# Layer 0's self-attention in steps of two head pairs: a decoder kernel on Trainium2

## The chip, the cores and the metric

The kernel runs on one core of a Trainium2 chip, in one launch. The metric is the device time in microseconds. A core has five engines, each with its own queue of instructions that it works off in order: TensorE (PE, matrix products and transposes, which write into the PSUM banks), VectorE (DVE), ScalarE (ACT), GpSimd (POOL) and SyncE (SP, which issues DMAs). Engines wait for each other through semaphores.

## The reference, cut to what matters

Two decoder layers work on x of 16 x 256 x 128 (batch, tokens, width), each with a self-attention, a cross-attention to a context of 64 tokens and a mixture-of-experts block. All is float32. The change is in layer 0's self-attention, of 16 heads of 64:

```python
x = x + attn(layernorm(x))          # layer 0, self-attention
q, k, v = (x @ W).reshape(b, n, 16, 64)     # for Wq, Wk, Wv
bias = slope[h] * (pos[:, None] - pos[None, :])
scores = einsum('bihd,bjhd->bhij', q, k) * 64**-0.5 + bias
scores = where(pos[:, None] >= pos[None, :], scores, -1e30)
out = einsum('bhij,bjhd->bihd', softmax(scores), v)
attn = out.reshape(b, n, 1024) @ Wo + bo
...
x = x + xattn(layernorm(x), ctx)    # layer 0, leaky ReLU, norm, softmax, gate
x = x + moe(layernorm(x))           # layer 0, 8 experts, 2 per token
...                                 # layer 1, the same three kinds
```

## The kernel before

The tokens stand in eight chunks of 512, which is two batches each. Layer 0's self-attention is one loop over *head pairs*: 16 batches of 8 pairs are 128 units, and the loop has 134 steps. For PE, DVE and ACT the order of the instructions is the order of the code; POOL and SP follow by the same order where nothing else is said.

The stages of a unit and their lines (of the kernel before):

- `qk_mm` (L395) projects q or k for two pairs, one of the two in each step, four steps ahead of the scores. The product lies in a bank of the pool `ps_m` (tag "m", three banks); `qk_out` (L406, ACT) copies it out.
- `scores` (L450, PE): two heads side by side, each on 64 of the array's 128 rows. A head has a bank of `ps_s` (four banks). Only the causal three 128 x 128 blocks are made: one of 128 columns, one of 256.
- `greatest` (L463, DVE): adds the bias strip, writes the sum to SBUF and finds the extreme of each row. One step behind the scores.
- `exponentials` (L475, ACT) with the row sums. In the same step as greatest.
- `scaled`: reciprocal (L484, DVE), then two multiplications per head (L486, POOL). Two steps behind the scores.
- `flip` (L497, PE): three transposes per head, into an "m" bank; `flipped` (L502, DVE) copies them to SBUF. Four steps behind.
- `values` (L512, PE): the two heads on 64 of the array's columns each, into the one bank of `ps_o`; `values_out` (L524, ACT) copies the pair's 256 columns. Five steps behind.

Between them stand, in an order by hand, other pieces: `v_mm` and `v_out` (L412 PE, L421 DVE; v for eight heads and half the tokens), `y_mm` and `y_out` (L427, L435; the output projection of the batch before), `turn` and `turned` (L131, L385; the transposed layernorm of the next chunk), `stats` (L340, L341), `normed` (L346, L348, L354 on POOL) and `biased` (L376, POOL). q, k, v, y, turned layernorms, flips and the front pieces all draw on the three "m" banks in turn.

The *front pieces* of a chunk are the cross-attention, the router and the shared expert of layer 0 (`front_pieces`, L620 to L835). Each is a pair of a function for PE (or none) and one for the other engines (`mm`, `post`). They are planned one to a step from step 16 c + 22 for chunk c, so that the 28 pieces of a chunk overlap with those of the next; the first centring is L365 on ACT, the scatter of rows for the experts is L790 on POOL. The last pieces (chunk 7, part of chunk 6) run in the experts' loop that follows. The core of a step before, by engine:

```python
scores(at(0)); values(at(5)); flip(at(4), 0); flip(at(4), 1)    # PE, behind the pieces
greatest(at(1), 0); scaled(at(2), 0)                            # DVE, POOL
scaled(at(2), 1); greatest(at(1), 1)
flipped(at(4), 0); flipped(at(4), 1)
exponentials(at(1), 0); exponentials(at(1), 1); values_out(at(5))   # ACT
```

Of the kernel before, what the change touches and what calls it, by code (L numbers as in the profile page):

```python
# [15 lines left out]
F32 = mybir.dt.float32  # L16
# [6 lines left out]
P = 128  # L23
# [39 lines left out]
def kernel(ctx: ExitStack, tc: tile.TileContext, a: dict, out: bass.AP):  # L63
# [174 lines left out]
    with ExitStack() as ph:  # L238
# [162 lines left out]
        def qk_out(g, which):  # L401
            dst = qk[g, which] = qkvp.tile(
                [P, 2, N], F32, tag="qk"[which], name=f"{'qk'[which]}0_{g}", bufs=3
            )
            scale = (-(DH**-0.5), 1.0)[which]
            nc.scalar.activation(dst, m_of.pop(("qk", g, which)), AF.Copy, scale=scale)  # L406
# [83 lines left out]
        def flip(u, i):  # L490
            b, h = u[0], 2 * u[1] + i
            pr = pr_of.pop((b, h))
            ps = tp_of[b, h] = ps_m.tile([P, 3 * P], F32, tag="m", name=f"t0_{b}_{h}")
            for blk in range(3):

                cols = slice(blk * P, (blk + 1) * P)
                nc.tensor.transpose(ps[:, cols], pr[:, cols], ident)  # L497

        def flipped(u, i):
            b, h = u[0], 2 * u[1] + i  # L500
            pT_of[b, h] = pp.tile([P, 3 * P], F32, tag="pT", name=f"pT0_{b}_{h}", bufs=5)
            nc.vector.tensor_copy(pT_of[b, h], tp_of.pop((b, h)))  # L502

        def values(u):
            b, pair = u
            po = o_of[u] = ps_o.tile([P, N], F32, tag="o", name=f"o0_{b}_{pair}")
            v = vals[b, pair // 4]
            for jt, c0 in ((0, 0), (1, P)):
                for h in (2 * pair, 2 * pair + 1):
                    rows = slice((h % 2) * DH, (h % 2 + 1) * DH)  # L510
                    pT = pT_of[b, h]
                    nc.tensor.matmul(  # L512
                        po[rows, c0:N], v[:, jt, h % 8 * DH : (h % 8 + 1) * DH],
                        pT[:, 0:N] if jt == 0 else pT[:, N:],
                        start=(jt == 0), stop=(jt == 1),
                    )
            for h in (2 * pair, 2 * pair + 1):
                del pT_of[b, h]

        def values_out(u):  # L520
            b, pair = u
            if pair == 0:
                oT[b] = qkvp.tile([P, NPAIR, N], F32, tag="oT", name=f"oT0_{b}", bufs=1)
            nc.scalar.copy(oT[b][:, pair, :], o_of.pop(u))  # L524

# [68 lines left out]
        def front_pieces(c):  # L594
# [239 lines left out]
            def p_sdown():  # L834
                nc.vector.tensor_tensor(x[c], x[c], g.pop("sy"), ALU.add)  # L835

            first_part = [
                (None, lambda: stats(c, 0, "x0")),
                (None, lambda: stats(c, 2, "x0")),
                (None, lambda: root(c, "x0")),  # L840
                (None, p_centred),
                (mm_turn, p_turned),
                (mm_scores, p_leaky),
# [9 lines left out]
                (None, lambda: stats(c, 0, "f0")),  # L853
                (None, lambda: stats(c, 2, "f0")),
                (None, p_root2),
                (None, p_centred2),
                (mm_turn2, p_turned2),
                (mm_logits, p_logits),
# [84 lines left out]
        def early_pieces():  # L943
            def table():
                tiles_of("num_a", P - 1)
                starts_of("start_a", tabled["num_a"])

            def table2():
                start = tabled["start_a"]
                row = list(entries(tab_a, EARLY, start, None))[-1]  # L950
                nc.vector.tensor_copy(tab_a[:, 1, :], row)

                done = tabled["done"] = new("done", (P, E))
                nc.vector.tensor_scalar(done, start, -1.0, float(EARLY), ALU.mult, ALU.add)
# [36 lines left out]
        with tc.manual_schedule(engines=ordered):  # L991
            for t0 in (0, 2):
                stats(0, t0)
            normed(0, nc.vector)
            bias_strips()
            biased(0)
            turn(0)
            turned(0)
            for g in range(2):
                for which in range(2):  # L1000
                    qk_mm(g, which)
                    qk_out(g, which)
            front_constants()

            units = [(b, p) for b in range(B) for p in range(NPAIR)]
            n = len(units)
            side = {}  # L1010

            def plan(first, pieces):
                for k, piece in enumerate(pieces):
                    side.setdefault(first + k, []).append(piece)

            plan(17, [(lambda h=h: ctx_turn(h), lambda h=h: ctx_turned(h)) for h in range(2)])
            for c in range(NCHUNK):
                first_step = 16 * c + 22
                plan(first_step, front_pieces(c))
                if c == EARLY_C - 1:  # L1020
                    plan(first_step + 24, early_pieces())
                if c == NCHUNK - 1:
                    plan(first_step + 25, late_pieces())
            steps = 8 * (B - 1) + 14
            for i in range(steps):
                b, p = divmod(i, NPAIR)

                def at(lag):
                    return units[i - lag] if 0 <= i - lag < n else None

                pieces = []
                if i + 4 < n:
                    key = ((i + 4) // 2, i % 2)
                    pieces.append((lambda: qk_mm(*key), None, lambda: qk_out(*key)))
                if b < B and p in (2, 3, 6, 7):
                    vkey = (b, p // 4, p % 2)
                    pieces.append((lambda: v_mm(*vkey), lambda: v_out(*vkey), None))
                if p == 5 and 1 <= b <= B:
                    pieces.append((lambda: y_mm(b - 1), lambda: y_out(b - 1), None))
                if p == 7 and b % 2 == 0 and b // 2 + 1 < NCHUNK:  # L1040
                    c = b // 2 + 1
                    pieces.append((lambda: turn(c), None, lambda: turned(c)))
                more = side.get(i, [])

                for mm, _, _ in pieces:
                    mm()
                if at(0):
                    scores(at(0))
                if at(5):
                    values(at(5))  # L1050
                if at(4):
                    flip(at(4), 0)
                    flip(at(4), 1)
                for mm, _ in more:
                    if mm:
                        mm()

                if at(1):
                    greatest(at(1), 0)
                if at(2):  # L1060
                    scaled(at(2), 0)
                for _, out_v, _ in pieces:
                    if out_v:
                        out_v()
                if at(2):
                    scaled(at(2), 1)
                if at(1):
                    greatest(at(1), 1)
                if at(4):
                    flipped(at(4), 0)  # L1070
                    flipped(at(4), 1)
                if b % 2 == 0 and b // 2 + 1 < NCHUNK:
                    if p in (1, 3):
                        stats(b // 2 + 1, p - 1)
                    elif p == 4:
                        normed(b // 2 + 1)
                    elif p == 6:
                        biased(b // 2 + 1)

                if at(1):  # L1080
                    exponentials(at(1), 0)
                for _, _, out_a in pieces:
                    if out_a:
                        out_a()
                if at(1):
                    exponentials(at(1), 1)
                if at(5):
                    values_out(at(5))
                for _, post in more:
                    post()  # L1090


    pending = []
# [1073 lines left out]
```

## Time and profile before

| what | value |
|---|---|
| median of 3 runs | 1544.63 us (1543.79 to 1545.28) |
| the profiled execution | 1540.27 us |
| its span, first to last instruction | 1538.6 us |
| PE busy | 1461.4 us, 95% |
| DVE, ACT, POOL busy | 1175.6, 971.1, 667.9 us |
| mean granted PE clock | 0.982 |
| first and last scores of the attention (L450) | 18.0 us, 625.7 us |

The profile is of one execution. A row of the timeline gives the start, the time until the end of the last instruction merged in it, the engine, the line, the operation with its tiles (output <- inputs), the shape and the count; in brackets stands how long the engine was idle before it and what ended that. Matmuls are pipelined, so the distance of two starts tells what one costs, and the duration does not. PEld is PE's loading of weights.

A row of the view by stretches gives the stretch, its length, then the busy time and the number of instructions of PE, PEld, DVE, ACT and POOL, the granted clock, the share of the DMA engines and their GB/s.

### The profile page before, as it was taken

The page shows a single profiled execution, that of the slowest core. Times are in us where ns is not written, and L with a number is a line of the kernel's source. Part 1 is how long each engine was busy: PE and PEld are TensorE (multiplying, and loading weights), DVE is VectorE, ACT ScalarE, POOL GpSimd, SP SyncE. Part 2 cuts the span into 40 slices and gives each one's busy share as a digit, 9 for nine tenths or more (in the row PEclk, how much of TensorE's full clock was granted, in tenths as well). Part 3 has the DMA queues.
Part 4 walks back from the last instruction along what each step waited for, and adds up shares of the span by engine and source line. Part 5 has one row for each costly group of instructions (what it writes and reads, how often), then busy time and mean ns, then how long its engine had stood idle before and what let it go on. Part 6 is the DMA issues. An engine that isn't in the chain of part 4 may idle for free.

```text
span 1538.6 us, 34876 instructions
## 1 busy us (share of the span) xinstructions
PE 1461.4 (95%) x11569; PEld 1069.0 (69%) x11569; DVE 1175.6 (76%) x4620; ACT 971.1 (63%) x2619; POOL 667.9 (43%) x1102
## 2 busy tenths in 40 slices
PE   7999999999999999899999899999999996899897
PEld 4666666666666666689999777777777764565564
DVE  6666666667676767677878779999999978888863
ACT  5666565656565656354333368888888884767752
POOL 7354646464747464555533311101101015657643
PEclk9999999999999999999999989999999997999999
DMA  7760000000000000457777300000000000122122
GB/s 220 249 202 1 1 14 3 9 8 5 12 1 15 1 15 1 133 172 235 224 237 236 100 22 9 15 15 9 15 1 2 2 1 1 29 53 53 36 62 49
DMA packets 76321, 95.01 MB, mean 62 GB/s; under 512 B 15936, under 2 KB 59200, under 8 KB 76144
## 3 DMA queue, kind: packets, MB, share of 16 engines
q1 hardware_dynamic: 61312, 45.59, 10.9%
q10 hardware_dynamic: 10512, 38.28, 7.7%
q0 software_dynamic: 4320, 8.92, 1.7%
q8 instruction: 94, 1.54, 0.4%
q14 instruction: 83, 0.68, 0.1%
HBM read 64.11 MB, written 28.65 MB: 60 GB/s over the span
## 4 chain that ended last, share of the span: by engine, by line
PE 81%; DVE 12%; ACT 3%; issue 2%; DMA 1%; POOL 0%; POOLq 0%; ACTq 0%; SPq 0%; DVEq 0%
PE t L1659 7%; PE pqk L395 7%; PE s L450 6%; PE o L512 6%; PE t L497 5%; PE s L1627 5%; PE g L1298 4%; PE o L1674 4%; PE y L427 4%; PE y L1316 4%; PE u L1298 4%; PE pv L412 3%; PE pqk L1540 3%; PE yf L2035 2%; PE tx L1889 2%
## 5 line engine op out<-in xcount | busy, mean ns | idle before, releaser
L475 ACT ACTIVATE p<-p,nm 128x128 f32<-128x128 f32 (+1 forms) x512 | 227.5, 446 | 183.9 <-DVE nm L463 174.9
L486 POOL TENSOR_SCALAR p<-p,rs 128x128 f32<-128x128 f32 (+1 forms) x512 | 213.7, 434 | 187.3 <-DVE rs L484 159.4
L1649 ACT ACTIVATE p<-p,nm 128x256 f32<-128x256 f32 x512 | 225.7, 508 | 37.5 <-DVE nm L1638 35.2
L502 DVE COPY pT<-t 128x384 f32<-128x384 f32 x256 | 131.0, 553 | 102.4 <-PE t L497 102.3
L1638 DVE CUSTOM_DVE_ANT_0 p<-s,strip 128x256 f32<-128x256 f32 x512 | 188.1, 419 | 18.3 <-PE s L1627 17.8
L463 DVE CUSTOM_DVE_ANT_0 p<-s,strip 128x128 f32<-128x128 f32 (+1 forms) x512 | 158.1, 346 | 1.3 <-PE s L450 1.3
L1659 PEld LDWEIGHTS t<-ident,p 128*128 128x128 f32 x1024 | 111.2, 142 | 47.4 <-issue 12.6
L1659 PE MATMUL t<-ident,p 128*128 128x128 f32 x1024 | 141.5, 282 | 0.0
L1326 POOL DMA_INDIRECT rows_out<-yr,to x71 | 68.7, 967 | 117.3 <-DVE yr L1325 109.2
L1505 POOL TENSOR_SCALAR ve_a<-mv_a 128x2 f32<-128x2 f32 x16 | 3.7, 231 | 265.0 <-DVE mv_a L1500 264.9
L450 PE MATMUL s<-k,q 64*128 64x128 f32 (+1 forms) x1024 | 118.5, 350 | 0.0
L512 PE MATMUL o<-pT,v 128*64 128x256 f32 (+1 forms) x1024 | 112.8, 340 | 0.8 <-DVE pT L502 0.8
L497 PE MATMUL t<-ident,p 128*128 128x128 f32 x768 | 113.3, 283 | 0.2 <-ACT k L406 0.2
L450 PEld LDWEIGHTS s<-k,q 64*128 64x128 f32 x1024 | 67.0, 186 | 62.5 <-issue 56.3
L512 PEld LDWEIGHTS o<-pT,v 128*64 128x64 f32 x1024 | 62.9, 136 | 61.6 <-issue 25.9
L497 PEld LDWEIGHTS t<-ident,p 128*128 128x128 f32 x768 | 82.1, 141 | 23.2 <-issue 15.4
L475 ACT ACTIVATION_READ_ACCUMULATOR p<-p,nm 128x1 f32 x512 | 96.5, 188 | 0.0
L1306 ACT ACTIVATE gs<-gs 128x512 f32<-128x512 f32 x71 | 44.7, 630 | 77.0 <-DVE gs L1305 64.9
L1667 DVE COPY pT<-t 128x512 f32<-128x512 f32 x128 | 88.1, 688 | 6.2 <-PE t L1659 3.2
L1627 PE MATMUL s<-k,q 32*128 32x256 f32 x1024 | 85.3, 408 | 0.6 <-DVE nm L1638 0.5
L421 DVE COPY v<-pv 128x512 f32<-128x512 f32 x64 | 44.0, 687 | 50.8 <-PE pv L412 50.8
L790 POOL DMA_INDIRECT rows_in<-xn,slot_in x64 | 64.2, 1004 | 33.8 <-DVE nm L463 20.5
(338 smaller groups left out, 3487.8 us busy)
## 6 DMA issues: line engine op xcount, KB each, us to landing
gu<-in_L_ffn_gate_up_w ACTq DMA_DIRECT2D x71, 512.0 KB
rows_in<-zero SPq DMA_DIRECT2D x131, 130.0 KB
spread<-wrows SPq DMA_DIRECT2D x16, 512.0 KB
xr<-rows_in SPq DMA_DIRECT2D x71, 65.0 KB
y<-rows_out SPq DMA_DIRECT2D x16, 256.0 KB
x<-in_x SPq DMA_DIRECT2D x8, 256.0 KB
out_x<-yo SPq DMA_DIRECT2D x16, 128.0 KB
rows_out<-yr,to POOLq DMA_INDIRECT x71, 3.7
```

The source lines that it names most:

```text
L450: nc.tensor.matmul(ps_of[b, h][:, cols], q[rows, u2, iq], k[rows, u2, 0:nk], start=True, stop=True,)
L463: nc.vector.tensor_tensor_reduce(out=pr[:, cols], in0=ps[:, cols], in1=strip[:, h, P : 2 * P] if it == 0 else strip[:, h, :], scale=1.0, s ...
L475: nc.scalar.activation(pr[:, cols], pr[:, cols], AF.Exp, bias=nm[:, it : it + 1], scale=-1.0, accum_out=sm[:, it : it + 1],)
L486: nc.gpsimd.tensor_scalar(pr[:, cols], pr[:, cols], rs[:, it : it + 1], 1.0, ALU.mult, ALU.mult)
L497: nc.tensor.transpose(ps[:, cols], pr[:, cols], ident)
L502: nc.vector.tensor_copy(pT_of[b, h], tp_of.pop((b, h)))
L512: nc.tensor.matmul(po[rows, c0:N], v[:, jt, h % 8 * DH : (h % 8 + 1) * DH], pT[:, 0:N] if jt == 0 else pT[:, N:], start=(jt == 0), stop=(j ...
L1298: nc.tensor.matmul(ps[:, f, :], gu[:, lo + f * P : lo + (f + 1) * P], xT, start=True, stop=True,)
L1627: nc.tensor.matmul(ps_of[b, h][:, it, :], q[rows, g, it * P : (it + 1) * P], k[rows, g, :], start=True, stop=True,)
L1638: nc.vector.tensor_tensor_reduce(out=pr[:, it, :], in0=ps[:, it, :], in1=strip1[:, h, (1 - it) * P : (1 - it) * P + N], scale=1.0, scalar= ...
L1649: nc.scalar.activation(pr[:, it, :], pr[:, it, :], AF.Exp, bias=nm[:, it : it + 1], scale=-1.0)
L1659: nc.tensor.transpose(ps[:, jt, it * P : (it + 1) * P], pr[:, it, jt * P : (jt + 1) * P], ident,)
```

## The change

A step now takes two head pairs, that is four heads, and the loop has 67 steps. Both projections of q and k of the next but one step come first; then the scores of both pairs; then the first front piece, the v, y or turn pieces; then the values of the pairs of two steps ago, into two halves of one bank, copied out by one instruction; then the flips of the four heads of the step before, into banks of `ps_s` in place of "m"; then the second front piece. Greatest and exponentials of the four heads are done in the step of their scores, with the copies of q and k between them; scaled and flipped are one step behind. Two no-op pieces are added to the front pieces of the chunks 0 to 4, one for 5 and 6. The early table of the experts is planned one place later.

```diff
         def flip(u, i):
...
-            ps = tp_of[b, h] = ps_m.tile([P, 3 * P], F32, tag="m", name=f"t0_{b}_{h}")
+            ps = tp_of[b, h] = ps_s.tile([P, 4 * P], F32, tag="s", name=f"t0_{b}_{h}")
...
         def values(u):
             b, pair = u
-            po = o_of[u] = ps_o.tile([P, N], F32, tag="o", name=f"o0_{b}_{pair}")
+            if pair % 2 == 0:
+                o_of[b, pair // 2] = ps_o.tile([P, 2, N], F32, tag="o", name=f"o0_{b}_{pair}")
+            po = o_of[b, pair // 2][:, pair % 2, :]
...
-            nc.scalar.copy(oT[b][:, pair, :], o_of.pop(u))
+            nc.scalar.copy(oT[b][:, 2 * two : 2 * two + 2, :], o_of.pop((b, two)))
...
+            wait = [], [(None, lambda: None)]
             first_part = [
                 (None, lambda: stats(c, 0, "x0")),
                 (None, lambda: stats(c, 2, "x0")),
                 (None, lambda: root(c, "x0")),
+                *wait[c <= EARLY_C],
                 (None, p_centred),
...
                 (None, p_root2),
+                *wait[c < EARLY_C - 1],
                 (None, p_centred2),
...
-                    plan(first_step + 24, early_pieces())
+                    plan(first_step + 25, early_pieces())
...
-            for i in range(steps):
-                b, p = divmod(i, NPAIR)
+            for j in range(steps // 2):
+                b, p = divmod(2 * j, NPAIR)
...
+                for mm, _, _ in pieces[0:2]:
+                    mm()
+                for u in at(0):
+                    scores(u)
+                run(0, 0)
+                for mm, _, _ in pieces[2:]:
+                    mm()
+                for u in at(2):
+                    values(u)
+
+                for u, k in before_them:
+                    scaled(u, k)
+                outs = [out for _, _, out in pieces if out]
+                for n in range(4):
+                    if heads:
+                        greatest(*heads[n])
+                        exponentials(*heads[n])
+                    if n < 3 and outs:
+                        outs.pop(0)()
+                run(0, 1)
+                for _, out_v, _ in pieces:
+                    if out_v:
+                        out_v()
+                for u in at(2)[0:1]:
+                    values_out(u[0], u[1] // 2)
+
+                for u, k in before_them:
+                    flip(u, k)
+                run(1, 0)
+                for u, k in before_them:
+                    flipped(u, k)
...
+                run(1, 1)
```

`at(lag)` gives the two units of `lag` double steps ago, `heads` are the four heads of this step, `before_them` those of the step before; `run(k, 0)` issues the PE part of the front piece k of the step, `run(k, 1)` its other part. `pieces[0:2]` are the two q/k projections, as long as there are any.

More of the change, by code (lines that the diff above doesn't have):

```diff
@@ L501, in flipped @@
             pT_of[b, h] = pp.tile([P, 3 * P], F32, tag="pT", name=f"pT0_{b}_{h}", bufs=5)
-            nc.vector.tensor_copy(pT_of[b, h], tp_of.pop((b, h)))
+            nc.vector.tensor_copy(pT_of[b, h], tp_of.pop((b, h))[:, 0 : 3 * P])
         def values(u):
             b, pair = u
-            po = o_of[u] = ps_o.tile([P, N], F32, tag="o", name=f"o0_{b}_{pair}")
+            if pair % 2 == 0:
+                o_of[b, pair // 2] = ps_o.tile([P, 2, N], F32, tag="o", name=f"o0_{b}_{pair}")
+            po = o_of[b, pair // 2][:, pair % 2, :]
             v = vals[b, pair // 4]
@@ L518, in values, with values_out @@
                 del pT_of[b, h]
-        def values_out(u):
-            b, pair = u
-            if pair == 0:
+        def values_out(b, two):
+            if two == 0:
                 oT[b] = qkvp.tile([P, NPAIR, N], F32, tag="oT", name=f"oT0_{b}", bufs=1)
-            nc.scalar.copy(oT[b][:, pair, :], o_of.pop(u))
+            nc.scalar.copy(oT[b][:, 2 * two : 2 * two + 2, :], o_of.pop((b, two)))
         ctxT = wpool.tile([P, B * S], F32, tag="ctxT", name="ctxT")
@@ L1008 @@
             units = [(b, p) for b in range(B) for p in range(NPAIR)]
-            n = len(units)
             side = {}
@@ L1024 @@
             steps = 8 * (B - 1) + 14
-            for i in range(steps):
-                b, p = divmod(i, NPAIR)
+            for j in range(steps // 2):
+                b, p = divmod(2 * j, NPAIR)
                 def at(lag):
-                    return units[i - lag] if 0 <= i - lag < n else None
+                    k = 2 * (j - lag)
+                    return units[k : k + 2] if 0 <= k < len(units) else []
+                heads = [(u, k) for u in at(0) for k in range(2)]
+                before_them = [(u, k) for u in at(1) for k in range(2)]
@@ L1031 @@
                 pieces = []
[L1032 to L1038, printed above, removed]
+                if 2 * j + 4 < len(units):
+                    for which in range(2):
+                        key = (j + 2, which)
+                        pieces.append(
+                            (lambda key=key: qk_mm(*key), None, lambda key=key: qk_out(*key))
+                        )
@@ L1039 @@
+                if b < B and p in (2, 6):
+                    for jt in range(2):
+                        key = (b, p // 4, jt)
+                        pieces.append(
+                            (lambda key=key: v_mm(*key), lambda key=key: v_out(*key), None)
+                        )
+                if p == 4 and 1 <= b <= B:
                     pieces.append((lambda: y_mm(b - 1), lambda: y_out(b - 1), None))
-                if p == 7 and b % 2 == 0 and b // 2 + 1 < NCHUNK:
+                if p == 6 and b % 2 == 0 and b // 2 + 1 < NCHUNK:
@@ L1041 @@
                     c = b // 2 + 1
                     pieces.append((lambda: turn(c), None, lambda: turned(c)))
-                more = side.get(i, [])
-                for mm, _, _ in pieces:
-                    mm()
[L1047 to L1061, printed above, removed]
+                more = [side.get(i, []) for i in (2 * j, 2 * j + 1)]
+                def run(k, part):
+                    for piece in more[k]:
+                        if piece[part]:
+                            piece[part]()
+                for mm, _, _ in pieces[0:2]:
+                    mm()
+                for u in at(0):
+                    scores(u)
@@ L1064 @@
                         out_v()
[L1065 to L1071, printed above, removed]
+                for u in at(2)[0:1]:
[5 more added lines that the diff above has]
+                    flipped(u, k)
                 if b % 2 == 0 and b // 2 + 1 < NCHUNK:
-                    if p in (1, 3):
-                        stats(b // 2 + 1, p - 1)
+                    c = b // 2 + 1
+                    if p in (0, 2):
+                        stats(c, p)
                     elif p == 4:
[L1076 to L1090, printed above, removed]
+                        normed(c)
+                    else:
+                        biased(c)
+                run(1, 1)
     pending = []
```

## The prediction

> **What bounds the kernel now.** I read the page first: engines, then the slices.
>
> ```profile
> PE 1461.4 (95%) x11569; PEld 1069.0 (69%) x11569; DVE 1175.6 (76%) x4620; ACT 971.1 (63%) x2619; POOL 667.9 (43%) x1102
> ...
> PE   7999999999999999899999899999999996899897
> ```
>
> TensorE (PE) is busy in almost every slice. The changed stage runs from the first scores (18.0 us, by the view of line L450) to 653.5 us (last row of the drain below): 635.5 us for 134 steps. "Busy" does not say that PE streams all the time, so the second view is the stretch between the output projections of two batches of one parity, which is one chunk (16 steps, one set of front pieces):
>
> ```profile
> 253.45:334.50 81.05, 79.69 (x571) 54.88 (x570) 56.19 (x268) 49.73 (x178) 47.26 (x89) 1.00 0.03 8
> ```
>
> 81.05 us, PE 79.69; VectorE (DVE) 56.19, ScalarE (ACT) 49.73, GpSimd (POOL) 47.26: all three have slack on average. The third view is the timeline of one step. Starts matter, not durations, since matmuls overlap:
>
> ```profile
> 299.89 0.28 DVE L463 CUSTOM_DVE_ANT_0 p<-s,strip 128x128 f32<-128x128 f32 x1
> ...
> 300.28 0.40 ACT L475 ACTIVATE p<-p,nm 128x128 f32<-128x128 f32 x1 [2.43 <-DVE nm L463]
> ...
> 300.42 0.93 PE L450 MATMUL s<-k,q 64*128 64x128 f32 x8
> ...
> 301.17 0.57 ACT L406 ACTIVATE q<-pqk 128x512 f32<-128x512 f32 x1
> ...
> 301.28 0.87 PE L512 MATMUL o<-pT,v 128*64 128x256 f32 x8
> ...
> 301.65 0.39 ACT L475 ACTIVATE p<-p,nm 128x128 f32<-128x128 f32 x1
> ...
> 302.08 0.88 PE L497 MATMUL t<-ident,p 128*128 128x128 f32 x6
> ...
> 302.66 1.02 DVE L502 COPY pT<-t 128x384 f32<-128x384 f32 x2 [0.83 <-PE t L497]
> ...
> 302.70 0.83 POOL L486 TENSOR_SCALAR p<-p,rs 128x128 f32<-128x128 f32 x2
> 302.79 1.03 PE L395 MATMUL pqk<-xnT,wk 128*128 128x256 f32 x4
> ...
> 303.66 1.02 PE L412 MATMUL pv<-wv,xnT 128*128 128x512 f32 x2
> ...
> 304.61 0.52 PEld L450 LDWEIGHTS s<-k,q 64*128 64x128 f32 x8 [0.76 <-issue]
> ```
>
> Four q/k instructions of 256 columns take 303.66 - 302.79 = 0.87, 0.217 each. At that rate scores and values, whose instructions run two at a time on half the array, need 3 x 0.217 = 0.65 each, the six 128-column transposes 0.65, the values projection 0.87. Start to start they take 0.86, 0.80, 0.71 and 0.95: **0.50 us per step is lost to changing the array's shape** (0.21 + 0.15 + 0.06 + 0.08). So PE's own order bounds this stage; real waits are few. The same timeline has two in a chunk, 0.72 us before tp_f and 0.64 us before pqk, both for a work bank ("m") that ACT empties: 1.4 us.
>
> **The change, by its parts.** T is the start of a double step on PE; E0 to E6 and O0 to O6 are the double steps of an even or odd batch that begin with pair 0, 2, 4, 6.
>
> *Fewer changes of shape.* 16 steps of 0.50 are 8.0 us per chunk. Eight double steps pay it once, 4.0; in seven of them a projection or front piece now stands between scores and values, at 0.1 more (re-entering, as the 0.08 above). That saves 3.3. If the slow first scores instruction comes back with the second pair (0.1), it is 2.5; I take 2.9. Without waits a chunk is then 81.05 - 1.4 - 2.9 = 76.75.
>
> *What becomes shorter between engines.* Exponentials, scaling and flip were one, two and four steps behind the scores; now they are zero, one and one double step behind. The timetable of a double step: q/k T to T+1.74; scores from 1.82, first pair to 2.68, second to 3.33. The first greatest (DVE) can start with the first 128 columns, T+2.35; ACT starts 0.39 after it (299.89 to 300.28), needs 0.89 per head (300.28 to 301.17) plus 0.17 here, since the second part waits for the 256 columns, and then copies q: 3.80 to 4.37. After 0.48 of that copy (301.17 to 301.65) head 1 goes to 5.17, k is copied to 5.74, heads 2 and 3 end at 6.5 and 7.4. So q's work bank is free at T+4.4, k's at T+5.8. There are three such banks, and PE, in order, wants the third and the next at T+3.33:
>
> - O2, O6, E2, E6: the first values projection has the third bank (3.33 to 4.2), the second waits for q's: 0.2 in O2, O6, E6. In E6 the layernorm turn then waits from 5.27 for k's: 0.5.
> - O4: logits 3.33 to 4.25, context scores wait to 4.4 (0.15) and end at 5.05, the output projection waits to 5.8: 0.9 together.
> - E2: shared-up to 4.2; the gate's first bank 0.2, its second from 4.85 to 5.8: 1.15 together.
> - O2: centring now stands in the same double step as its turn. ACT finishes heads at 7.4, then two groups of four centring activations of 1.65 each (the group's row in the timeline of ACT), to 9.1 and 10.7. PE reaches the turns at 3.33 + 1.74 + 0.2 + 0.1 + 1.4 values + 1.4 flips = 8.2 and waits 0.95, turns 0.43, and waits 1.15: 2.1. Next behind them is the whole of O4.
> - O0: DVE ends E6 with the copies of the flips (two in 1.02), 1.1 after PE, and four layernorm statistics of 0.41, so the reciprocals are done at T+3.2. POOL scales a head in 0.83 (302.70), done at 3.8 to 6.3; the flips start at 4.8 and take 0.33: the third and fourth wait 0.7 together. In E0 and E4 I find none.
>
> Sum 0.6 + 0.5 + 0.9 + 1.15 + 2.1 + 0.7 = **6.0 us of new waits per chunk**, against the 1.4 that go. Bounds: 1.5 (each new wait no longer than the old ones) to 12 (each twice as long, because a late DVE delays ACT and that the bank).
>
> *Clock.* In the trace waits of 0.7 us leave the clock at 1.00 (the chunk's row); only 3.10 us of idle in the drain (below) is followed by slow instructions, 2.07 for a pair that takes 1.02 elsewhere. My longest wait is 1.2, so I charge nothing.
> The Trainium skill, "TensorE: Matmul & The Clock Gate", section "A second HAM failure mode: psum-queue depth-cycling", speaks against this change: it tells of a kernel that cycled through banks, idled briefly between groups and lost its clock again and again. By its half-rate window of about 3.4 us an estimate would be 1.7 us more per event, some 24 us for two events in each of seven chunks, and the sum would be 1577; no row here shows it.
>
> *Flips in the score banks.* Same count of transposes. Scores of the next step wait for the copies out (DVE): the last ends 1.1 after the flips, the second pair's scores start 2.5 after them: covered by the q/k projections and the first scores; where those are gone (the last two double steps with scores) 0.4 each. A flip also waits for this step's greatest (0.55 a head, done at 2.9 to 4.6); values run until 4.8, so it is covered. *Copy of values*: one of 512 columns for two of 256 (0.57 for 2 x 0.35): ACT only, which has 31 us of slack per chunk: nothing. *No-op pieces* move front pieces by one or two places and issue nothing; the chunk's row scatters on POOL come two places later, in E0 and E2, where POOL has time before the next scaling. No load or SP queue changes place. POOL's layernorm (four rows of 0.90 and a power of 1.04) and bias add stand behind the scaling in E4 and E6, with 5 us to spare.
>
> *Fill and drain.* At the start the flips of the first two pairs, with the second values projection waiting for its bank, come some 1 us behind. At the end PE now idles:
>
> ```profile
> 629.90 0.88 PE L497 MATMUL t<-ident,p 128*128 128x128 f32 x6
> 633.88 2.07 PE L817 MATMUL su<-xT,sgu 128*128 128x512 f32 x2 [3.10 <-DVE rs L669]
> ...
> 648.52 1.24 PE L512 MATMUL o<-pT,v 128*64 128x256 f32 x8 [0.41 <-DVE pT L502]
> 649.69 3.84 PE L427 MATMUL y<-wo,oT 128*128 128x128 f32 x32
> ```
>
> From 627.6 to 653.5 single pairs trickle through: 26 us for 17.6 us of work (five values 4.0, four pairs of flips 2.9, front pieces 7.1, y 3.6). With two fewer hand-overs I take 3 us less (0 to 6).
>
> **Sum.** A chunk: 76.75 + 6.0 = 82.75, 1.7 more. Front pieces run in steps 22 to 134, seven chunks: +12. The 22 steps before (about 1.1 chunks after the fill) have only the waits of v and turn, 1.3, so -1.6 each: -2. Fill +1, drain -3. Together +8. The profiled execution took 1540.27 (span 1538.6) and would take 1548; the median of the runs is 4.4 higher, so 1544.63 + 8 = **1552.6 us**.
>
> **Rivals.**
> (1) *The switches win: faster.* Break-even is at 4.3 us of new waits per chunk, with the -4 at the ends at 4.9. Below it the change gains: with the turns' 2.1 gone and the rest halved (2.0 left) a chunk is 78.75, -16 over seven, -4 at the ends: 1525; with no waits 1511. For it: the three other engines have 25 us or more of slack per chunk, and one wait can swallow the next one. Against: ACT's order within a step is fixed, and 4.4 against 3.33 is no average. Place: the work banks; it decides from a wait under 0.6 us per double step.
> (2) *POOL paces the flips: much slower.* If the flips wait in one more double step per batch as in O0 but from the first head, 4 x (0.83 - 0.33) = 2.0 us by 14 batches: +28, 1580. For it: scaling had two steps of lead and has now half of one. Against: POOL's 47.26 of 81.05.
> (3) *A wash*: the terms cancel within 0.2% (3 us, about what a measurement of this kernel can tell): 1544.6. Partly the change then would not do what it says, the pieces put between scores and values taking back what the double step saves.
>
> **Chances.** Forecast (1548 to 1568) 0.42, rival 1 0.34, rival 2 0.14 (from 1568 up), rival 3 0.10. So faster 0.34, same 0.10, slower 0.56. The range takes rival 1 down to waits of 1.5 us per chunk at 7 x (78.25 - 81.05) = -20 and -4 at the ends, 1520, and rival 2 to 1580; about a tenth is left out on each side. The likeliest case alone is 1548 to 1568.
>
> **What would show it.** Right: between two output projections of one parity about 82.8 us; PE's waits led by work banks (q, k out of L406) and by the turn of the second layernorm waiting for ACT; about three us less per chunk lost between groups of instructions. Wrong: the chunk under 80 us, or the longest waits at the flips (POOL, L486) or scores (copies out). The drain after the last scores should be under 23 us. The later stages should keep their lengths.

## The result, and the profile after

The changed kernel takes 1572.47 us (median of six runs, 1568.08 to 1573.76) against 1544.87 us of the kernel before (six runs, 1543.68 to 1545.68): a ratio of 1.0172, interval [1.0157, 1.0188], or 27.6 us more. Slower was forecast, but by 8 us; 1572 lies outside the likeliest case (1548 to 1568) and inside the range. The profiled execution took 1568.32 us, its span is 1566.6. The page's engine row and the slices:

```profile
PE 1463.5 (93%) x11569; PEld 1079.4 (69%) x11569; DVE 1176.7 (75%) x4620; ACT 959.6 (61%) x2555; POOL 656.7 (42%) x1102
...
PE   6999999999999999899999989999999996899987
```

The engines are busy as long as before or less (PE 2 us more, ACT and POOL 11 less). So the 28 us are nearly all waits. The starts of the output projections (L427) make a ruler on which both traces can be laid; all in us:

| stretch | before | after | more | forecast |
|---|---|---|---|---|
| start to the fifth output projection | 210.9 | 214.7 | +3.8 | about +1 |
| fifth to thirteenth, four chunks | 324.5 | 336.2 | +11.7 | +7 |
| thirteenth to the last scores | 90.3 | 90.2 | -0.1 | about +3 |
| drain: last scores to the attention's end | 27.8 | 31.1 | +3.3 | -3 |
| the attention's end to the experts' 25th tile | 82.0 | 87.6 | +5.6 | 0 |
| to layer 1's first output projection | 206.2 | 206.1 | -0.1 | 0 |
| layer 1 from there | 596.9 | 600.7 | +3.8 | 0 |

The forecast's column is the prediction's sum laid out by its steps (fill +1, the 22 first steps -2, 1.7 per chunk, drain -3). The attention took 18.7 us more where 8 were forecast, and 9 us lie behind it, where nothing was. In the first stretch 2.6 of the 3.8 us lie ahead of the first output projection (60.97 before, 63.60 after).

The view by stretches of the changed kernel, first the four chunks, then the drain; the last row is the drain of the kernel before:

```profile
214.67:550.90 336.23, 322.85 (x2274) 223.42 (x2272) 223.25 (x1060) 193.57 (x681) 181.65 (x352) 1.00 0.02 8
641.00:672.20 31.20, 23.84 (x156) 16.26 (x152) 20.33 (x79) 7.48 (x23) 16.80 (x26) 0.84 0.44 133
625.70:653.50 27.80, 23.86 (x154) 16.28 (x152) 17.55 (x60) 7.84 (x26) 14.62 (x22) 0.88 0.59 178
```

A chunk is 336.23 / 4 = 84.06 us, 82.75 were forecast. The granted clock is 1.00 in the chunks and 0.84 in the drain, where it was 0.88 before. PE is busy for 23.84 us of the drain, as before (23.86): what the drain lost is waits. The two longest of them, from the timeline of the changed kernel:

```profile
651.63 1.02 PE L665 MATMUL sm<-half_of,ex 128*128 128x2 f32 x4 [3.50 <-ACT ex L660]
...
657.08 3.54 PE L498 MATMUL t<-ident,p 128*128 128x128 f32 x12 [1.68 <-POOL p L486]
```

Now one double step of the changed kernel, O2, from its timeline (many rows of the other engines left out). T, E and O are those of the prediction; T is 281.97:

```profile
281.97 1.03 PE L395 MATMUL pqk<-xnT,wq 128*128 128x256 f32 x4
...
283.80 1.58 PE L450 MATMUL s<-k,q 64*128 64x128 f32 x16
284.86 0.29 DVE L463 CUSTOM_DVE_ANT_0 p<-s,strip 128x128 f32<-128x128 f32 x1 [1.87 <-PE s L450]
...
285.20 0.40 ACT L475 ACTIVATE p<-p,nm 128x128 f32<-128x128 f32 x1 [2.26 <-DVE nm L463]
285.31 1.13 PE L412 MATMUL pv<-wv,xnT 128*128 128x512 f32 x2
...
286.09 0.58 ACT L406 ACTIVATE q<-pqk 128x512 f32<-128x512 f32 x1
...
286.72 1.13 PE L412 MATMUL pv<-wv,xnT 128*128 128x512 f32 x2 [0.28 <-ACT q L406]
...
287.44 0.58 ACT L406 ACTIVATE k<-pqk 128x512 f32<-128x512 f32 x1
...
289.67 1.64 ACT L365 ACTIVATE xn<-x,nb_f,rstd_f 128x128 f32<-128x128 f32 x4
...
290.59 1.11 PE L131 MATMUL tp_f<-ident,xn 128*128 128x128 f32 x4
291.21 1.64 ACT L365 ACTIVATE xn<-x,nb_x,rstd_x 128x128 f32<-128x128 f32 x4
...
291.75 1.48 PE L131 MATMUL tp_x<-ident,xn 128*128 128x128 f32 x4
...
293.07 1.03 PE L395 MATMUL pqk<-xnT,wq 128*128 128x256 f32 x4
```

The two named mechanisms are there. The second values projection waits for the bank that q's copy empties: 286.72 - 285.31 = 1.41 for an instruction pair of 0.87. The turns follow the centring tile by tile, 1.16 and 1.32 where 0.43 is the work; since each tile waits a little, no bracket of these PE rows shows it, and only the distance of the starts does. Scores of both pairs take 285.31 - 283.80 = 1.51: the slow first instruction comes once, not twice (the prediction took half of that, 0.4 of 0.8 us per chunk).

### The profile page after: what moved, and what is told of

It is laid out like the page before. It is cut to its first block, busy times and chain, and to the rows that moved or that the text cites. A ratio compares the mean times of both kernels' runs of the same rounds, so it can differ in the third digit from the quotient of the medians.

```text
span 1566.6 us, 34946 instructions
## 1 busy us (share of the span) xinstructions
PE 1463.5 (93%) x11569; PEld 1079.4 (69%) x11569; DVE 1176.7 (75%) x4620; ACT 959.6 (61%) x2555; POOL 656.7 (42%) x1102
## 4 chain that ended last, share of the span: by engine, by line
PE 70%; DVE 14%; ACT 8%; POOL 4%; issue 3%; DMA 1%; ACTq 0%; POOLq 0%; SPq 0%; DVEq 0%
PE t L1673 8%; PE pqk L395 6%; PE s L1641 5%; PE t L498 4%; PE o L1688 4%; PE o L515 4%; ACT p L475 4%; PE y L427 4%; PE g L1312 4%; PE u L1312 4%; PE y L1330 3%; PE s L450 3%; POOL p L486 3%; PE pqk L1554 3%; PE yf L2049 2%
## 5 line engine op out<-in xcount | busy, mean ns | idle before, releaser
L486 POOL TENSOR_SCALAR p<-p,rs 128x128 f32<-128x128 f32 (+1 forms) x512 | 207.3, 425 | 113.4 <-DVE rs L484 111.8
L463 DVE CUSTOM_DVE_ANT_0 p<-s,strip 128x128 f32<-128x128 f32 (+1 forms) x512 | 147.6, 353 | 84.4 <-PE s L450 70.3
L503 DVE COPY pT<-t 128x384 f32<-128x384 f32 x256 | 127.7, 552 | 62.9 <-PE t L498 62.3
L1673 PE MATMUL t<-ident,p 128*128 128x128 f32 x1024 | 141.5, 282 | 0.0
L498 PE MATMUL t<-ident,p 128*128 128x128 f32 x768 | 109.2, 284 | 4.7 <-POOL p L486 1.7
L450 PE MATMUL s<-k,q 64*128 64x128 f32 (+1 forms) x1024 | 101.2, 337 | 0.0
L515 PE MATMUL o<-pT,v 128*64 128x256 f32 (+1 forms) x1024 | 98.6, 335 | 0.0
L450 PEld LDWEIGHTS s<-k,q 64*128 64x128 f32 x1024 | 72.6, 187 | 24.3 <-issue 7.6
L1641 PE MATMUL s<-k,q 32*128 32x256 f32 x1024 | 84.9, 408 | 0.5 <-DVE nm L1652 0.5
L412 PE MATMUL pv<-wv,xnT 128*128 128x512 f32 x128 | 70.2, 639 | 10.7 <-ACT q L406 10.0
```

Source lines behind the costliest of these rows:

```text
L450: nc.tensor.matmul(ps_of[b, h][:, cols], q[rows, u2, iq], k[rows, u2, 0:nk], start=True, stop=True,)
L463: nc.vector.tensor_tensor_reduce(out=pr[:, cols], in0=ps[:, cols], in1=strip[:, h, P : 2 * P] if it == 0 else strip[:, h, :], scale=1.0, s ...
L486: nc.gpsimd.tensor_scalar(pr[:, cols], pr[:, cols], rs[:, it : it + 1], 1.0, ALU.mult, ALU.mult)
L503: nc.vector.tensor_copy(pT_of[b, h], tp_of.pop((b, h))[:, 0 : 3 * P])
L515: nc.tensor.matmul(po[rows, c0:N], v[:, jt, h % 8 * DH : (h % 8 + 1) * DH], pT[:, 0:N] if jt == 0 else pT[:, N:], start=(jt == 0), stop=(j ...
L1641: nc.tensor.matmul(ps_of[b, h][:, it, :], q[rows, g, it * P : (it + 1) * P], k[rows, g, :], start=True, stop=True,)
```

## The experiments

Theory A: the changes of shape save what was forecast, and waits take it back, for work banks behind exponentials (e1), for centring (e2), for GpSimd's scaling (e3). Rival: PE's new order is itself dearer. Theory C: the experts' loop lives on the lead of its weight loads (e5, e6). Theory D: the front pieces beside the experts' first tiles stand one place later (e10). Ratios are to the kernel before, run beside each. The table gives the four chunks' mean from the same two output projections, and the drain to the last output projection's end:

| kernel | time, us | ratio, interval | chunk | drain |
|---|---|---|---|---|
| before | 1544.87 | 1 | 81.1 | 27.8 |
| after | 1572.47 | 1.0172 [1.0157, 1.0188] | 84.06 | 31.1 |
| e1 copies first | 1542.0 | 0.9975 [0.9958, 0.9993] | 80.28 | 31.8 |
| e2 centring earlier | 1568.5 | 1.0135 [1.0108, 1.0161] | 82.82 | 31.6 |
| e3 scaling at the step's end | 1570.14 | 1.0145 [1.0119, 1.0172] | 82.68 | 37.3 |
| e4 all three | 1534.13 | 0.9921 [0.9892, 0.9949] | 78.50 | 37.4 |
| e5 before, table 3 steps later | 1556.98 | 1.0069 [1.0048, 1.0089] | 81.1 | 30.4 |
| e6 e4, table earlier | 1538.64 | 0.9953 [0.994, 0.9966] | 78.48 | 36.3 |
| e7 e4, values split | 1547.0 | 1.0006 [0.9996, 1.0017] | 80.06 | 32.3 |
| e8 e6, values ahead | 1533.84 | 0.9919 [0.9895, 0.9942] | 78.04 | 37.1 |
| e9 after, last scaling on DVE | 1585.03 | 1.011 [1.008, 1.014] | 85.1 | 31.6 |
| e10 before, one place later | 1572.03 | 1.0037 [1.002, 1.0054] | 82.7 | 29.3 |
| e11 e4, values ahead | 1548.24 | 0.9883 [0.986, 0.9906] | 79.5 | 31.7 |
| e12 e11, last scaling on DVE | 1546.55 | 0.9866 [0.9842, 0.9889] | 79.4 | 29.8 |

e9 to e12 ran on a chip on which the kernel before takes 1567.99 us; their times and chunks stand beside the others by ratio only.

### e1: the copies of q and k ahead of the exponentials

```diff
+for out in outs[0:2]:
+    out()
+outs = outs[2:]
 for n in range(4):      # greatest, exponentials of the four heads
```

> The changed kernel, with the copies of q and k ahead of the four heads' greatest and exponentials instead of between them. Theory A (most of the loss is PE waiting, in order, for a work bank that ACT empties behind the exponentials): the chunk of 84 us loses the 5 us of waits in front of v, turn, gate, context scores and y that the trace shows, seven chunks and the first batches make 37 us: 1535 us. Rival B (the short chain from exponentials to the flips is the bound, and a freed bank only moves the wait to the flips): less than 15 us, above 1557.

30 us less than the changed kernel, and below the kernel before. In the timeline of e1, the same double step:

```profile
270.09 0.60 ACT L406 ACTIVATE q<-pqk 128x512 f32<-128x512 f32 x1 [1.09 <-PE pqk L395]
270.85 1.58 PE L450 MATMUL s<-k,q 64*128 64x128 f32 x16
270.95 0.60 ACT L406 ACTIVATE k<-pqk 128x512 f32<-128x512 f32 x1 [0.27 <-PE pqk L395]
...
272.25 0.40 ACT L475 ACTIVATE p<-p,nm 128x128 f32<-128x128 f32 x1 [0.70 <-DVE nm L463]
272.36 1.98 PE L412 MATMUL pv<-wv,xnT 128*128 128x512 f32 x4
```

Both copies lie in time in which ACT had waited for DVE, so the exponentials start no later (T + 3.23 in both; T is 269.02 here), and the four instructions of the values projection run as one row. The wait for banks is shown as the largest part: 84.06 - 80.28 = 3.8 us per chunk.

### e2: centring one piece earlier

```diff
-    *wait[c <= EARLY_C],
     (None, p_centred),
+    *wait[c <= EARLY_C],
...
-    *wait[c < EARLY_C - 1],
     (None, p_centred2),
+    *wait[c < EARLY_C - 1],
```

> The changed kernel, with the no-op piece behind each centring instead of ahead of it, so that the centring of both layernorms (ACT) stands one place before the double step that turns them. Theory A: the two turns lose their 1.8 us of waiting for ACT per chunk, some 12 us over seven chunks: 1560. Rival (ACT is as late one place earlier, since the centring then waits for the roots on POOL and holds up the next exponentials): no gain, 1570 to 1575.

1.24 us per chunk, less than the turns cost. The turns of O2 are 0.44 and 0.43 us from start to start now, so they no longer wait. But ACT's centring of eight tiles went into another's way: in O2 of e2 the values projection waits longer for its bank.

```profile
286.95 1.12 PE L412 MATMUL pv<-wv,xnT 128*128 128x512 f32 x2 [1.00 <-ACT q L406]
```

### e3: scaling at the end of the heads' own step

`scaled` for the four heads stands behind `flipped`, in the step of their scores, ahead of the second front piece's other part.

> The changed kernel, with the reciprocals and multiplications of a step's heads at the end of that step, behind the copies of the flips and ahead of the layernorm statistics and the second front piece, instead of at the start of the next. Theory A (in two of eight double steps DVE's tail and what POOL does before the scaling make the flips wait, 1.17 and 0.94 us in the trace): 2.1 us per chunk go, 15 us: 1557. Rival B (the whole chain is the bound): DVE now waits there for the last exponential, and the time does not fall: 1570 or more.

The chunk loses 1.38 us, as flips on POOL's pace go; 2.1 were expected. That is some 10 us over seven chunks, but the ratio gives only 4, where 15 were expected. The drain takes 6 us back: by its bracket the last copy of values on ACT now stands behind a wait for the experts' gathered rows (timeline of e3, and a stretch of it):

```profile
667.41 0.58 ACT L526 COPY oT<-o 128x512 f32<-128x512 f32 x1 [3.17 <-DMA xr<-rows_in]
...
668.05 4.64 PE L427 MATMUL y<-wo,oT 128*128 128x128 f32 x20 [3.59 <-ACT oT L526]
...
668.00:672.70 4.70, 4.64 (x20) 4.34 (x20) 0.00 (x0) 0.00 (x0) 0.00 (x0) 0.50 0.87 273
```

Behind the wait of 3.59 us PE runs at a granted clock of 0.50: 20 instructions take 4.64 us, where 32 take 3.84 in both kernels, which is 2.40 for 20. Wait and slow clock together are 5.8 of the 6.1 us.

### e4: all three

> All three edits together. Theory A: the savings add up but for what they share: 35 + 12 + 15 us less, 1510, well below the kernel before (1545), whose 16 changes of shape per chunk it halves. Rival B: no better than the best of the three.

1534.13: faster than the kernel before, 24 us short of what was expected. The chunk falls by 5.56, not by 3.78 + 1.24 + 1.38 = 6.4; one wait hides another. PE's remaining waits in a chunk of e4 (timeline, rows with an idle time in 245.61 to 324.01):

```profile
272.09 1.12 PE L412 MATMUL pv<-wv,xnT 128*128 128x512 f32 x2 [0.78 <-ACT q L406]
...
302.02 0.61 PE L665 MATMUL sm<-half_of,ex 128*128 128x2 f32 x4 [1.00 <-ACT ex L660]
...
308.23 1.13 PE L395 MATMUL pqk<-xnT,wk 128*128 128x256 f32 x4 [0.19 <-DVE gs L813]
```

Together 1.97. Without them the chunk would be 78.50 - 1.97 = 76.5, or a little less, since brackets understate (the first row's start comes 1.04 us late, going by starts): the prediction's base was 76.75. Most of the miss lies in the chunks. The three runs' expectations make 5 + 1.8 + 2.1 = 8.9 per chunk, and 5.56 came. The drain takes 6.3 us back, with the same copy and the same slow clock as in e3, and the experts' loop gives nothing.

### e5: the kernel before with the early table three steps later

```diff
-plan(first_step + 24, early_pieces())
+plan(first_step + 27, early_pieces())
```

> The kernel before, with the early table of the experts planned three steps later (27 in place of 24) and nothing else. Theory C (the experts' loop begins on the lead of its weight loads: the first load comes 1.1 us after the table, 19.6 us ahead of the last output projection in the kernel before and 15.9 in the changed one, and the loop's 25th tile then stands 82.0 and 87.6 us behind that projection): the attention keeps its length (653.5), the first load comes some 8 us later, and the time from the end of the attention to the 25th tile grows by 5 to 10 us: 1550 to 1555. Rival D (the loads have time to spare and the 5.5 us in the changed kernel are those of other pieces moved by one place): no change, 1545.

0.69%, 10.6 us more. The first weights of the experts are loaded 14 us later, and PE stands still for them (timeline of e5):

```profile
662.76 2.07 PE L1298 MATMUL g<-xTs,gu 128*128 128x128 f32 x8 [6.54 <-DMA gu<-in_L_ffn_gate_up_w]
```

So theory C holds at a lead of 7.3 us (first load to the attention's end). The changed kernel has 15.9 where the kernel before has 19.6, and there PE waits for no weight load.

### e6: e4 with the early table where the kernel before has it

> The three edits together (copies first, centring early, scaling at the tail), and the early table planned one place earlier, as in the kernel before (24 for 25). Theory C: the first load comes some 5 us earlier (12 in place of 16 behind the last scores) and the 25th tile stands 87 in place of 93 us behind the attention: 1528, 5 to 6 less than with the three edits. Rival D: as with the three edits, 1534.

A miss: not below e4. With 20.2 us of lead the experts' first 24 intervals take 84.9 us against e4's 85.6. The lead is not what the experts' loop of the changed kernel lacks.

### e7: e4 with the values of the two pairs apart

```diff
-for u in at(2): values(u)
+for u in at(2)[0:1]: values(u)
...
+for u, k in before_them[0:2]: flip(u, k)
+for u in at(2)[1:2]: values(u)
-for u, k in before_them: flip(u, k)
+for u, k in before_them[2:]: flip(u, k)
```

> The three edits, with the flips of the first two heads between the values of the two pairs: the same instructions, two more changes of the array's shape in each double step. Theory A (a change of shape costs what the starts in the trace of before say: 0.15 from values to flips, 0.06 in the flips, 0.15 back into values): 0.3 us per double step, 2.4 per chunk of 78.5, 20 us in all: 1554. Rival E (the saving of the double step is not in the changes of shape but in fewer waits): no more than 5 us.

0.85% above e4, 13 us. The chunk grows by 80.06 - 78.50 = 1.56, 0.195 per double step, for one more entry into values and one more into flips. The prediction read 0.15 + 0.06 = 0.21 for these two from the kernel before. The expectation of this run (2.4 per chunk, 1554) counted a third change and missed. The changes of shape cost what was read.

### e8: e6 with the values ahead of the pieces

`values` of both pairs directly behind the scores, then the front piece and the projections.

> As e6, with the values directly behind the scores, ahead of the front piece and the v, y and turn pieces: one change of shape less in seven of eight double steps. Theory A: 0.1 us for each, 0.7 per chunk, 5 us in all below e6, as long as the work banks are free by then: 1523. Rival: the pieces now reach the flips' POOL and the copies closer, no gain.

0.34% below e6, 5 us; the chunk 0.44 less, 0.05 per double step, for the re-entry that the prediction put at 0.1.

### e9: the last four heads scaled by VectorE

```diff
+on = nc.vector if b == 15 and u[1] >= 6 else nc.gpsimd
 for it, cols in PARTS:
-    nc.gpsimd.tensor_scalar(
+    on.tensor_scalar(
```

> The changed kernel, but the probabilities of the very last four heads are scaled by VectorE in place of GpSimd. In the changed kernel's drain eight row scatters stand on GpSimd ahead of this scaling (646.65 to 656.6 us) and the last flips begin at 657.08. Theory (GpSimd's order paces the drain): the flips begin behind the last sums and values, at about 653.6, and go at PE's pace, so the attention ends 5 us earlier (26 instead of 31 us from the last scores to its end), about 1567. Rival (PE's own chain of hand-overs and ScalarE's late exponentials pace the drain): within 1.5 us of the changed kernel, 1571 or more.

The expectation comes from the chain of waits in the changed kernel's drain, a few rows of which are:

```profile
by line: POOL rows_in L792 24.5%; PE y L427 11.8%; PE t L498 11.1%; issue 9.5%; PE pre L691 6.0%; DVE p L463 5.1%; PE o L515 4.5%; PE pre L698 4.0%; PE sy L831 3.6%; DVE gs L826 2.2%; DVE gs L825 1.9%; DVE seen L767 1.8%; DVE pT L503 1.7%; 
...
646.65 1.10 POOL rows_in L792
...
655.65 0.96 POOL rows_in L792
656.65 0.39 POOL p L486
657.08 3.56 PE t L498 x12
```

Eight scatters, then the scaling, then the flips, 16.0 us behind the last scores. In e9's timeline they start after 658.75 - 645.0 = 13.75 us, and the drain is still 31.6:

```profile
655.57 0.61 PE L666 MATMUL sm<-half_of,ex 128*128 128x2 f32 x4 [3.50 <-ACT ex L661]
...
658.75 1.97 PE L499 MATMUL t<-ident,p 128*128 128x128 f32 x12
...
662.03 1.95 DVE L504 COPY pT<-t 128x384 f32<-128x384 f32 x4
...
665.43 1.16 PE L832 MATMUL sy<-sdn,gs 128*128 128x128 f32 x8 [2.62 <-DVE gs L827]
```

The copies of the flips begin 3.3 us after the flips, since DVE works off the early table first, and the shared expert waits for DVE. The wait changed its owner. The rival holds for the drain. The ratio is below that of the changed kernel by 0.6%, on another chip; the drain does not explain that, and the cause stays open.

### e10: the kernel before with one no-op piece in the chunks 5 and 6

```diff
     (None, lambda: root(c, "x0")),
+    *([(None, lambda: None)] if c in (5, 6) else []),
     (None, p_centred),
```

> The kernel before, with one no-op piece ahead of the first centring of the chunks 5 and 6, as the change has it there; nothing else is changed. Theory (the front pieces that run beside the experts' first tiles stand one place later there, and that costs the experts' loop its 5 us): from the first to the 25th expert tile 85 to 86 us instead of 80.4, total about 1550. Rival (the loop's loss comes from what the attention's drain hands over late, not from the pieces' places): 80 to 81 us, total 1545.

0.37%, 5.8 us by the ratio [3.1, 8.5], as theory D expected. The first 24 intervals from one expert tile to the next take 88.2 us, more than the 85 to 86 expected (before 80.4, on another chip). One wait of it is the same in the changed kernel, where it comes at 708.23 (timeline of e10, with rows of a later stall):

```profile
702.28 0.61 PE L663 MATMUL sm<-half_of,ex 128*128 128x2 f32 x4 [1.25 <-ACT ex L658]
...
719.77 0.27 PE L1299 MATMUL g<-xTs,gu 128*128 128x128 f32 x1 [0.35 <-issue]
720.50 0.48 PE L1299 MATMUL g<-xTs,gu 128*128 128x128 f32 x2 [0.46 <-issue]
721.94 0.27 PE L1299 MATMUL g<-xTs,gu 128*128 128x128 f32 x1 [0.95 <-issue]
```

The first thirteen intervals take 50.5 us, against 48.0 in the kernel before and 51.2 in the changed kernel: 2.5 us of the 3.3 that the changed kernel loses there are lost here with the moved places alone, though on another chip. The fourteenth is 5.3 us longer than before, a stall put down to "issue", which e9, e11 and e12 on that chip show too (4.1 to 5.0); elsewhere the changed kernel and e1 stall 1.4 and 2.9 us one interval later, for gathered tiles that ACT delivers late, and the kernel before does not. No trace of the kernel before was taken on that chip. So the sign and the size of the total are shown; what makes up its second half is not.

### e11 and e12: the best version

e11 is e4 with the values ahead and the table where the change has it; e12 scales the last four heads on VectorE as well.

> The changed kernel with the three moves of e4 (copies of q and k ahead of the exponentials, centring one piece earlier, scaling at the step's own end) and the values directly behind the scores, ahead of the pieces; the early table stays where the changed kernel has it. If the earlier table of e6 and e8 really cost the 4.5 us by which e6 lost to e4: 1529 to 1530. If those 4.5 us were scatter from run to run: 1534.

> As e11, and the last four heads scaled by VectorE as in e9. If GpSimd paces the drain: 5 us under e11, about 1525 to 1529. If not: the same as e11 within 1.5 us.

0.9883 [0.986, 0.9906] and 0.9866 [0.9842, 0.9889]: by 1544.87 that is 1527 and 1524. Both beat both kernels. That e11 lies 0.36% below e8 speaks for the later table, but they ran on two chips and the intervals overlap; in e6 the trace put its loss against e4 into layer 1 (602.3 us against 597.7), not at the table. This stays open. e12 against e11 is within both intervals; its drain is 29.8 against 31.7, 2 us of the 5 expected.

## Why the prediction was right and wrong

The forecast was +8 us, and 28 came. By the table the misses are the drain (6.3 us), the experts' loop (5.6), the waits in the four chunks (4.7), layer 1 (3.8) and the start (2.8); the stretch up to the last scores was 3 us better than forecast.

**Right: what the changes of shape cost.** 0.50 per step was read from starts. e7 pays two of the four again, 0.195 against 0.21 read, and e4 less its waits is 76.5 against 76.75.

**Right in kind, too small: the waits.** 84.06 - 76.5 = 7.5 us per chunk, 6.0 were forecast. By terms, which add up to 3.8 + 1.6 + 2.1 = 7.5:

- Work banks: 0.6 + 0.5 + 0.9 + 1.15 = 3.15 forecast, 3.8 measured (e1). The step that failed is "can start with the first 128 columns, T+2.35": greatest started when the first pair was complete, T + 2.89, the exponentials at T + 3.23, and q's bank came free at 286.67, T + 4.70 instead of 4.4, k's at 288.02, T + 6.05 instead of 5.8. A values projection then waits 0.54, not 0.2.
- Turns: 2.1 forecast; 1.16 + 1.32 - 0.86 = 1.6 in the rows of O2, 1.24 by e2, which gave part of it to a bank.
- Flips on POOL: 0.7 in O0 and "none" in E0 forecast (0.7 is a slip: done at 3.8 to 6.3 and 0.33 each, only the fourth flip waits, 0.5). From the start of the flips to the next row on PE it is 2.54 in O0 and 2.31 in E0, where 1.36 is the work (289.23 to 290.59 in O2): 1.2 and 0.95, together 2.1, of which e3 wins 1.38. The step that failed is to take POOL in code order. POOL's rows in O0 and E0 of the changed kernel, with PE's flips:

```profile
277.00 1.04 POOL L348 TENSOR_TENSOR rstd_f<-ve_f,nhalf 128x4 f32<-128x4 f32 x1
278.12 0.19 POOL L346 TENSOR_SCALAR ve_x<-mv_x 128x4 f32<-128x4 f32 x1
278.41 3.23 POOL L486 TENSOR_SCALAR p<-p,rs 128x128 f32<-128x128 f32 x8
...
279.43 2.71 PE L498 MATMUL t<-ident,p 128*128 128x128 f32 x12
...
318.31 1.12 POOL L792 DMA_INDIRECT rows_in<-xn,slot_in  x1 [6.83 <-DVE rs L484]
319.48 3.23 POOL L486 TENSOR_SCALAR p<-p,rs 128x128 f32<-128x128 f32 x8
...
320.73 2.47 PE L498 MATMUL t<-ident,p 128*128 128x128 f32 x12
```

The layernorm's root and a row scatter run ahead of the scaling. They stand later in the code, but run sooner: the kernel fixes by hand the order of PE, DVE and ACT in this loop (`tc.manual_schedule`), not that of POOL. The flips then go at POOL's 0.8 a head.

**Wrong: the steps without front pieces.** I took 2 us off the first 22 steps, with waits of v and turn alone at 1.3 per chunk. They gained nothing: from the first to the second output projection, ahead of the first front piece, it is 35.1 us before and after. e1 makes it 33.0, so here too the banks took it. The fill was to cost 1 us: from the first scores to the first output projection it is 42.95 us before, 44.77 after, and 42.15 in e1, which gives it back.

**Wrong: the drain**, -3 forecast, +3.3 measured. The step that failed is "With two fewer hand-overs I take 3 us less". PE's idle time in the drain grew from 3.9 to 7.4 us at the same busy time; the longest waits are the 3.50 for a front piece's exponentials on ACT and the 1.68 for the flips. That each hand-over now carries four heads, and that the eight scatters and the early table stand in it, was left out. e9 shows that GpSimd's scaling alone does not hold the drain; which of the others does was not tested one by one.

**Wrong: "The later stages should keep their lengths."** The experts' loop lost 5.6. The no-op pieces were said to issue nothing, which is so, but for the chunks 5 and 6 they move pieces to other tiles of the experts' loop: e10 has this in the kernel before at 5.8 [3.1, 8.5] in total, and the traces agree for the first thirteen intervals only. Layer 1's +3.8 cannot be put down to the change: with its code untouched it takes 595 to 605 us over all these kernels, 604.4 in e5, which has the attention of before.

**Right: no clock term.** The chunks' granted clock is 1.00 with 7.5 us of waits in each, and the drain's lower clock (0.84, 0.88 before) leaves PE's busy time there as it was. In e3 and e4 the clock does cost time in the drain. The cycle that the Trainium skill tells of ("TensorE: Matmul & The Clock Gate", section "A second HAM failure mode: psum-queue depth-cycling") did not come about here; the estimate of 1577 worked out from that page would have been near the result for a reason that the trace excludes. **Right too:** the flips in the score banks delay no scores while there are projections ahead of them (their start is 0.95 to 1.07 us behind that of k's projection in all 62 such double steps); PE has no idle time ahead of scores on the page:

```profile
L450 PE MATMUL s<-k,q 64*128 64x128 f32 (+1 forms) x1024 | 101.2, 337 | 0.0
```

**The rivals.** Rival 1 put its point of decision at the work banks, and e1 is that case: with the bank waits gone the change is faster. Rival 2's pace by POOL was real, at 1.4 us per chunk (2.1 by the rows) instead of 4.

## What to carry to other kernels

Where matrix instructions of several array shapes alternate, grouping them paid here what the starts in the timeline promised, but only with the copies that empty the work banks issued ahead of the longer work that the same group starts on that engine; three lines made a loss of 1.7% a gain of 0.25%. Take an engine's order from its trace, not from the code, where the kernel does not fix it, and count what stands ahead of each hand-over. An empty slot in a plan is not free if the plan's tail runs beside another loop: look up which instruction meets which.

## What the hardware showed unexpectedly

Two scores groups back to back pay the change of shape once (1.51 us for 16 instructions, 2 x 0.65 of streaming and 0.21). In the drain, waits of 3.50 and 1.68 us go with a granted clock of 0.50 from 651 to 660 us, and in e3 a wait of 3.59 us with 0.50 behind it, while 7.5 us of shorter waits in each chunk left it at 1.00. And chips differ by more than most of these edits: the kernel before takes 1545 to 1546 us on three sets of runs and 1568 on a fourth.
